# The seam between head attention and output attention: order of the first signs, extremes in three parts, a buffer cleared later, values in smaller first groups

## The chip, the core and the metric

The kernel runs on one core of a Trainium2 chip. The metric is the device time of one execution in microseconds (us); the median of several runs is compared. Engines: TensorE (PE in the profile, PEld its weight loads), VectorE (DVE), ScalarE (ACT), GpSimd (POOL) and SyncE (SP), the last two also issuing DMAs. Each engine takes its instructions from a queue in order.

## What is computed

Four graph layers over 4096 nodes with 64 features and a dense 4096 x 4096 matrix of edges. Each layer adds its result to x. The change lies in the first layer, a graph attention with eight heads of 32 features, whose results are joined and go through one more attention (the "output attention"):

```python
h = maximum(_layernorm(x), 0)
e_s = leaky_relu(f1[:, :, None] + f2[:, None, :], 0.2)      # per head
h_s = elu(softmax(where(mask, e_s, NEG)) @ Wh_s)            # six heads from h, two from intent embeddings
h = concatenate(heads)                                      # 4096 x 256
Who = h @ W_out                                             # 4096 x 64
o1, o2 = Who @ a_out[:64], Who @ a_out[64:]
e_o = leaky_relu(o1[:, None] + o2[None, :], 0.2)
x = x + tanh(softmax(where(mask, e_o, NEG)) @ Who)
```

The other three layers (a hyperbolic attention, a mean over neighbours, a weighted list of the last neighbours) follow.

## The kernel before, in words

Nodes lie in 32 blocks of 128 (NB = 32), a block on the 128 partitions. The kernel never forms the softmax matrix. Since leaky_relu has two slopes, exp(leaky_relu(s + t)) is one of two products of a factor of the row and a factor of the column, and the sign of s + t tells which. So for each pair of blocks `split_edges` (L1227 to L1257) makes a tile of signs `st` (two instructions on ACT, L1242, or now and then on DVE, L1236), masks the edges with it (B, L1248, DVE), and, except for "whole" pairs, takes the other edges (C, L1256, DVE). TensorE then multiplies B and C by the values, scaled with the column factors. For a whole pair it multiplies all edges and takes B off again with negated values.

*Heads.* Two halves of the target nodes, eight heads in each: 16 units. `finish_unit` (L1740) is a generator that turns a unit's sums into elu(...) in steps: transposes (L1751), the division (L1781, nm), Relu and Exp on ACT (L1786, L1787), elu's last step into x (L1788, DVE). After the fourth and the eighth head it also multiplies by W_out: for four groups of four blocks, transposes of x (L1037), their copies on ACT (L1038), `product` (L1797, pwho) and the addition to `who` on DVE (L1808). `who` holds, for each node, the 64 values, then o1 and o2. Behind the last unit the rest of its generator runs out, then `scores_row(1)` (L1518: pro, a transpose of o1 on TensorE, its copy ro on ACT, its store by SP) and `extremes(1)` (L1526: maximum and minimum of o2 and of the values of 16 blocks, four reductions, L1532, and a change of sign, L1533). `extremes(0)` ran earlier, inside the heads.

*Output attention.* Four units of 1024 target nodes; in each, eight mask tiles `mo` of four source blocks (L2204, loaded by SP, three buffers). Ahead of it, in a group of which `in_order()` keeps the order on each engine: psv, the sum of the values by four products with a matrix of ones (L2061); m3, the joined extremes (L2068); their maximum over partitions on POOL (omax, L1208); td and the two Exps of `fzo` (L2071 to L2073); scale factors; and `parts` (L2080), which for a quarter of the blocks (8) makes the values YB and YC as pairs of float16: a product on DVE (pzo, L2085), a copy on ACT (L2088), a difference on DVE (L2090), and for YB a second copy on ACT (L2093). `factors` (L2095) makes YD1 and YD2, which sum the denominators. `staggered` interleaves such streams a step at a time. Behind the group, YCn, the negated YC of the whole pairs, is made for all of them at once (L2136), and then `radii()` (L1847) prepares scalars of the next layer and clears MOV, a buffer of 128 x 4096 bfloat16 that the next layer fills (L1861, POOL). nto, the negated o2 that the signs need, is made for each half (L2057).

In the loop (L2194 to L2251) each mask tile takes two calls of `split_edges`, the edges in another code for the next layer (nmo, L2217, DVE, stored by POOL, L2220), the products of B, C or mo (L2229, acco) and those of the denominators (L2242, L2248, ddo).

What sets the order: outside `in_order()` a scheduler places the instructions of each engine by the order of issue and estimated times; `behind(...)` keeps what is in it after given instructions. Tiles come from pools with a fixed number of buffers: two for st and C, four for B, two for pzo, so a fifth B waits until TensorE is done with the first. In the schedule of before, twelve signs of the output attention stand on ACT among the last steps of the heads, and two of the four psv on TensorE stand between the transposes of the last unit and one between the last two pwho. MOV's clearing stands on POOL ahead of omax.

Of the kernel before, what the change touches and what calls it, by code (L numbers as in the profile page):

```python
# [10 lines left out]
F32 = mybir.dt.float32  # L11
# [830 lines left out]
def kernel(  # L842
# [235 lines left out]
    with ExitStack() as l0:  # L1078
# [199 lines left out]
        orow_d = [dram.tile([1, HW], F32, name="orow_d") for _ in halves]  # L1278
        mx = spool.tile([P, 2, 4], F32, name="mx")
        fz = lp.tile([P, 2, NB, NH], F32, name="fz")  # L1280
# [203 lines left out]
        with ExitStack() as ha:  # L1484
# [40 lines left out]

            def extremes(i):  # L1526

                t, v = who[:, halves[i], D + 1], who[:, halves[i], 0:D]
                for c, (part, of, ax) in enumerate(
                    ((t, ALU.max, AX.X), (t, ALU.min, AX.X), (v, ALU.max, AX.XY), (v, ALU.min, AX.XY))  # L1530
                ):
                    nc.vector.tensor_reduce(mx[:, i, c : c + 1], part, ax, of)  # L1532
                nc.vector.tensor_scalar(mx[:, i, 1::2], mx[:, i, 1::2], -1.0, None, ALU.mult)  # L1533

            pending = None
            for hf in range(2):
                if hf == 1:
# [8 lines left out]
                for hd in range(NH):  # L1546
# [61 lines left out]
                    for j0 in range(0, NB, 2):  # L1608
# [85 lines left out]
                        if hf == 1 and hd == 1 and j0 == NB // 2:  # L1694
                            with behind(*done_at):
                                scores_row(0)
                                extremes(0)
                    if first:
# [40 lines left out]

                    def finish_unit(hf=hf, hd=hd, ev=ev, fme=fme):  # L1740
                        wh = wn[:, hf * HB : (hf + 1) * HB, hd]

# [43 lines left out]
                        nc.scalar.activation(ng, nm, AF.Relu, scale=-1.0)  # L1786
                        nc.scalar.activation(ng, ng, AF.Exp, scale=-1.0)  # L1787
                        nc.vector.scalar_tensor_tensor(  # L1788
# [5 lines left out]
                        def product(bq):  # L1794
                            pw = ps.tile([P, GB, D + 2], F32, name="pwho", tag="misc")
                            for b in range(GB):
                                nc.tensor.matmul(  # L1797
                                    pw[:, b, :],
                                    lhsT=by_g[:, 3 - bq % 2, b * P : (b + 1) * P],
                                    rhs=rho[:, c, :],  # L1800
                                    start=True,
                                    stop=True,
                                )
                            ws = who[:, hf * HB + bq * GB : hf * HB + (bq + 1) * GB, :]
                            if c == 0:
                                nc.vector.tensor_copy(ws, pw)
                            else:
                                nc.vector.tensor_tensor(ws, ws, pw, ALU.add)  # L1808

                        for bq in range(NS):  # L1810
# [8 lines left out]
                            if bq:  # L1819
                                product(bq - 1)  # L1820
                        yield
                        product(NS - 1)

# [3 lines left out]
            with in_order():  # L1827
                scores_row(1)
                extremes(1)
        ea.close()  # L1830
# [16 lines left out]
        def radii():  # L1847

            nc.vector.scalar_tensor_tensor(rabs, rt, -1.0, rt, ALU.mult, ALU.max)
            nc.vector.reciprocal(sqc, rabs)  # L1850
            nc.vector.tensor_tensor(cc, rt, rt, ALU.mult)
            nc.vector.reciprocal(cc, cc)
            nc.vector.tensor_tensor(c2, cc, cc, ALU.mult)
            nc.vector.tensor_scalar(m2c, cc, -2.0, None, ALU.mult)
            nc.vector.tensor_scalar(s2c, sqc, math.sqrt(2.0) * DIST_S, None, ALU.mult)
            nc.vector.tensor_scalar(p2c, cc, 2.0, None, ALU.mult)
            nc.vector.tensor_scalar(cneg, cc, -1.0, None, ALU.mult)
            nc.vector.tensor_scalar(maxn, rabs, 1.0 - PROJ_EPS, None, ALU.mult)
            nc.vector.tensor_scalar(hrow, rabs, 0.5, None, ALU.mult)
            nc.vector.tensor_copy(ident16, ident)  # L1860
            nc.gpsimd.memset(MOV, 0.0)  # L1861

# [147 lines left out]
        with ExitStack() as ob:  # L2010
# [18 lines left out]
            nc.gpsimd.memset(YD1, 0.0)  # L2029
            nc.gpsimd.memset(YD2, 0.0)  # L2030
            aug = hp.tile([P, NB, C_EL + KX], F16, name="aug")
            meano = hp.tile([P, NK, 2, D], F16, name="meano")
# [23 lines left out]
            for bs in halves:  # L2056
                nc.vector.tensor_scalar(nto[:, bs], tcol[:, bs], -1.0, None, ALU.mult)  # L2057
            with in_order():
                psv = ps.tile([P, 8, D], F32, name="psv", tag="misc")
                for g in range(4):  # L2060
# [6 lines left out]
                    )  # L2067
                nc.vector.tensor_tensor(m3, mx[:, 0], mx[:, 1], ALU.max)  # L2068
                m3 = col_maxs(m3, 4, "omax", hp)
# [8 lines left out]

                def parts(g, i):

                    bs = slice(g * NB // 4, (g + 1) * NB // 4)
                    fq = work.tile([P, NB // 4], F32, name="fq", tag="fq")
                    nc.vector.tensor_scalar(fq, fz[:, i, bs], Qo, None, ALU.mult)
                    pz = work.tile([P, NB // 4, D], F32, name="pzo", tag="pzo")
                    nc.vector.tensor_tensor(pz, vals[:, bs], over(fq, D), ALU.mult)  # L2085
# [6 lines left out]
                    if i == 0:  # L2092
                        nc.scalar.activation(y[:, bs, 1], pz, AF.Copy, scale=LO)  # L2093
                        yield 1

                def factors(i):
# [9 lines left out]

                staggered(parts(0, 0), parts(0, 1), factors(0), factors(1))
                nc.vector.tensor_copy(YD2[:, :, 0:3], YD1[:, :, 3:6])
                for g in range(1, 4):
                    staggered(parts(g, 0), parts(g, 1))  # L2110
                nc.vector.tensor_scalar(
# [22 lines left out]

            YCn = hp.tile([P, NB // 8, 2, 2 * D], F16, name="YCn")
            prepared = nc.vector.tensor_scalar(  # L2136
                YCn,
                YC.rearrange("p (n i) s d -> p n i (s d)", i=2)[:, 1::4],
                -1.0,
                None,  # L2140
                ALU.mult,
            )

            with tc.issue_after(prepared.ins):
                radii()
# [47 lines left out]
            for u in range(4):  # L2193
# [8 lines left out]
                for q in range(NQ):  # L2202
# [3 lines left out]
                    for t in range(0, JT, 2):  # L2206
                        j0 = q * JT + t
                        edges = m[:, t : t + 2, :]
                        whole = j0 // 2 % 4 == 1
                        B, C = split_edges(  # L2210
                            work, srow[:, us], nto[:, j0 : j0 + 2], edges, j0, NB + 1, not whole, 4
                        )
                        B2.append(B)
                        if t:
                            with behind(*done_at):
# [3 lines left out]
                                )  # L2219
                                nc.gpsimd.dma_start(noedge_d[q][u // 2][:, :, hs], nm8)  # L2220
                        products = [(accB, YB[:, j0 : j0 + 2], B), (accC, YC[:, j0 : j0 + 2], C)]
# [997 lines left out]
```

## Time and profile before

| | |
|---|---|
| median of 3 runs | 1922.95 us (1919.16 to 1933.77) |
| profiled execution: its own time | 1918.57 us |
| its span, first to last instruction | 1916.8 us |
| mean granted TensorE clock | 0.962 |
| busy: PE, DVE, ACT, POOL | 1756.7, 1586.0, 1428.3, 120.4 us |
| last head product ends, first output product starts | 915.3, 948.4 us |
| last product of the output attention ends | 1134.7 us |

How to read it: a row of the timeline or of the chain begins with the start and the length in us; "x4" counts instructions, and "[7.73 <-ACT YBo L2093]" is idle time of the engine before the row and what ended it. Rows of the chain of work that ended last give time that the path spent in a step. Rows of waits read: who waited for whom, us in total, times, longest. A row of stretches has a pair of busy time and count for each engine, then the granted clock (1.00 is full rate), the busy share of the DMA engines and GB/s. Line numbers are those of the kernel before.

### The profile page before, as it was taken

How to read it: one execution, taken by the hardware profiler on the slowest of the kernel's cores; microseconds unless marked ns; L12 is line 12 of the kernel's file. 1: busy time of each engine (PE TensorE's matmuls, PEld its weight loads, DVE VectorE, ACT ScalarE, POOL GpSimd, SP SyncE). 2: the span in 40 equal slices, each digit the busy share in tenths (PEclk: the TensorE clock that was granted, in tenths of full speed). 3: DMA queues.
4: the chain of work that ended last, by engine and by line, in shares of the span. 5: the costliest groups of instructions: out<-in, count | busy, mean ns of one | idle time of the engine just before them, and what ended most of it. 6: DMA issues, size and time to landing. Idle time of an engine off the chain costs nothing.

```text
span 1916.8 us, 44651 instructions
## 1 busy us (share of the span) xinstructions
PE 1756.7 (92%) x19374; PEld 818.1 (43%) x19374; DVE 1586.0 (83%) x2457; ACT 1428.3 (75%) x1470; POOL 120.4 (6%) x204
## 2 busy tenths in 40 slices
PE   5889988999999999999699996999999998899998
PEld 3444444444444444444334441333333333455433
DVE  6769999999869987999668876888988777756687
ACT  3768888899878987999578977777777775324565
POOL 2000100010000000000111100000011121110000
PEclk8899999999999999999699996999999999899999
DMA  8956554535411110100455534455543210784496
GB/s 112 178 138 92 112 75 80 134 123 194 161 51 51 52 51 24 57 35 2 123 178 185 187 100 128 139 169 177 178 121 119 72 39 6 276 232 154 154 346 183
DMA packets 145978, 239.09 MB, mean 125 GB/s; under 512 B 16662, under 2 KB 106086, under 8 KB 140230
## 3 DMA queue, kind: packets, MB, share of 16 engines
q1 hardware_dynamic: 131244, 194.02, 30.8%
q0 software_dynamic: 14528, 42.13, 12.5%
q8 instruction: 153, 2.51, 0.5%
q14 instruction: 53, 0.43, 0.1%
HBM read 245.37 MB, written 49.46 MB: 154 GB/s over the span
## 4 chain that ended last, share of the span: by engine, by line
PE 57%; DVE 21%; ACT 13%; issue 6%; DMA 2%; POOL 0%; SPq 0%; DVEq 0%; ACTq 0%; POOLq 0%
PE accj L2443 9%; PE accC L1597 7%; ACT st L1242 7%; DVE B L1248 7%; PE acco L2229 6%; PE accB L1597 3%; PE pv L3022 3%; DVE st L1236 3%; PE pf L2433 3%; PE sacc L3046 3%; PE accD L1597 2%; PE pl L2377 2%; PE pu L2397 2%; PE accL L1597 2%; PE pl L2383 2%
## 5 line engine op out<-in xcount | busy, mean ns | idle before, releaser
L1242 ACT ACTIVATE st<-srow,nt 128x2048 int8<-128x2048 f32 x352 | 683.0, 1994 | 85.4 <-DVE B L1248 84.1
L1248 DVE TENSOR_TENSOR B<-st,mres 128x1024 int32<-128x1024 int32 x256 | 311.5, 1220 | 59.5 <-PE accC L1597 36.7
L1597 PE MATMUL accB<-B,ybh 128*32 128x512 fp8e4 x3072 | 256.0, 381 | 20.3 <-DVE B L1248 20.2
L1597 PEld LDWEIGHTS <-ybh 128*32 128x32 bf16 (+1 forms) x6656 | 179.2, 97 | 212.2 <-issue 55.4
L1597 PE MATMUL accC<-mres,ych 128*32 128x512 fp8e4 x2272 | 228.5, 380 | 0.0
L1597 PE MATMUL accC<-B,ycn 128*32 128x512 fp8e4 x2272 | 228.5, 380 | 0.0
L1597 PE MATMUL accD<-B,ybh 128*32 128x512 fp8e4 x2048 | 208.0, 382 | 2.1 <-DVE h L1733 2.1
L1236 DVE TENSOR_SCALAR st<-srow,nt 128x2048 uint8<-128x2048 f32 x160 | 205.3, 1284 | 1.8
L2443 PE MATMUL accj<-sg,who 128*64 128x512 f32 (+1 forms) x512 | 196.9, 614 | 5.1 <-DVE sg L2436 4.8
L2443 PE MATMUL acci<-sg,who 128*64 128x512 f32 (+1 forms) x512 | 196.8, 614 | 0.0
L2399 ACT ACTIVATE yt<-pu,consts 128x512 f32<-128x512 f32 x144 | 98.5, 686 | 99.2 <-PE pu L2398 95.0
L2388 ACT ACTIVATE sg<-pl,rb 128x512 f32<-128x512 f32 x256 | 160.9, 679 | 10.2 <-PE pl L2383 7.5
L1597 PEld LDWEIGHTS <-ych 128*32 128x32 f16 x4096 | 118.3, 97 | 116.7 <-issue 12.1
L1597 PE MATMUL accL<-B,ybh 128*32 128x512 fp8e4 x1536 | 156.8, 384 | 4.3 <-DVE h L1732 4.3
L972 DVE SCALAR_TENSOR_TENSOR raw<-raw 128x1024 f32<-128x1024 f32 x128 | 153.8, 1215 | 0.0
L1242 ACT ACTIVATE st<-srowo,nto 128x1024 int8<-128x1024 f32 x128 | 137.9, 1138 | 19.0 <-DVE B L1248 13.3
L1256 DVE TENSOR_TENSOR C<-B,mres 128x1024 int32<-128x1024 int32 x114 | 139.5, 1224 | 3.1
L3036 ACT ACTIVATE w3b<-pv 128x512 int16<-128x512 f32 x172 | 90.9, 596 | 55.7 <-ACT w3b L3036 23.2
L1597 PE MATMUL accC<-C,ych 128*32 128x512 fp8e4 x1824 | 124.9, 383 | 6.3 <-DVE C L1256 6.2
L2377 PE MATMUL pl<-nm,noid 128*128 128x512 fp8e4 x256 | 82.2, 389 | 16.3 <-ACT sg L2388 14.6
L1597 PEld LDWEIGHTS <-ycn 128*32 128x32 f16 x2272 | 66.7, 97 | 60.1 <-issue 1.0
L2417 DVE SCALAR_TENSOR_TENSOR yt<-sqy,yt 128x1024 f32<-128x1024 f32 x72 | 84.8, 1218 | 5.3 <-ACT sqy L2409 5.2
(540 smaller groups left out, 2721.2 us busy)
## 6 DMA issues: line engine op xcount, KB each, us to landing
raw<-in_adj_dram SPq DMA_DIRECT2D x128, 512.0 KB, 4.7
mo<-edges SPq DMA_DIRECT2D x32, 512.0 KB, 4.1
noedge<-nmo POOLq DMA_DIRECT2D x32, 512.0 KB, 3.6
nm<-noedge SPq DMA_DIRECT2D x64, 256.0 KB, 3.1
m<-edges SPq DMA_DIRECT2D x32, 512.0 KB, 6.2
srow<-srow_d SPq DMA_DIRECT2D x15, 1024.0 KB, 8.2
mres<-in_adj_dram POOLq DMA_DIRECT2D x8, 1024.0 KB, 36.0
edges<-in_adj_dram POOLq DMA_DIRECT2D x8, 1024.0 KB, 14.9
```

What stands on the lines that cost most here:

```text
L972: nc.vector.scalar_tensor_tensor(raw, raw, 0.0, raw, ALU.is_gt, ALU.not_equal, accum_out=bad[:, c : c + 1])
L1236: nc.vector.tensor_scalar(st[:, i, :].bitcast(U8), srow, negs[:, i : i + 1], EDGE, ALU.is_gt, ALU.mult)
L1242: nc.scalar.activation(st[:, i, :], srow, AF.Sign, bias=negs[:, i : i + 1], scale=-1.0)
L1248: nc.vector.tensor_tensor(B.bitcast(I32), st.bitcast(I32), edges.bitcast(I32), ALU.bitwise_and)
L1256: nc.vector.tensor_tensor(C.bitcast(I32), B.bitcast(I32), edges.bitcast(I32), ALU.bitwise_xor)
L1597: ins = nc.tensor.matmul(acc[k * O : (k + 1) * O, :], lhsT=values, rhs=moving(k), start=start, stop=stop,)
L2229: sums = nc.tensor.matmul(acc[k], lhsT=Y[:, i].rearrange("p s d -> p (s d)"), rhs=E[:, i, k * G : (k + 1) * G], start=j0 + i == 0, stop=ac ...
L2377: nc.tensor.matmul(pl, lhsT=noid, rhs=nm[:, b, :].bitcast(F8), start=True, stop=False)
L2388: nc.scalar.activation(sg[:, b0 + k, :], pl, AF.Sigmoid, bias=rb[:, j : j + 1], scale=1.0)
L2399: nc.scalar.activation(far[gi, gj][:, b, :], pu, AF.Sigmoid, bias=nb_t, scale=2.0 * DIST_K / (DIST_S * DIST_S),)
L2443: nc.tensor.matmul(acc[r : r + n, :], lhsT=XQ[:, src, cols], rhs=w, start=start, stop=stop)
L3036: nc.scalar.activation(wk, pvs[i, k], AF.Relu)
```

## The change

Six edits. The extremes of the second half are taken in two parts: of the first 12 of its blocks inside the last unit's `finish_unit`, ahead of its last product, and of the last 4 behind it; mx has three parts and m3 is a reduction over them. The first two calls of `split_edges` in the output attention come after the last Exp of the heads. psv comes after the last `product` and is taken out of the group that is kept in order. MOV is cleared in the second unit, behind the store of its first nmo. The first group of values is cut into blocks 0 to 1 and 2 to 7 (8 blocks in one before). YCn is made one pair of blocks at a time, behind the YC of its group, in place of all at once at the end, and `radii()` follows the last of them.

```diff
-            def extremes(i):
+            def extremes(i, bs):
-                t, v = who[:, halves[i], D + 1], who[:, halves[i], 0:D]
+                t, v = who[:, bs, D + 1], who[:, bs, 0:D]
...
-                        nc.scalar.activation(ng, ng, AF.Exp, scale=-1.0)
+                        relieved = nc.scalar.activation(ng, ng, AF.Exp, scale=-1.0)
+                        relieved_at[:] = [relieved.ins]
...
+                            last_product[:] = [made.ins]
...
                         yield
+                        if final:
+                            extremes(1, slice(HB, NB - GB))
                         product(NS - 1)
...
             with in_order():
                 scores_row(1)
-                extremes(1)
+                extremes(2, slice(NB - GB, NB))
+            at_end = (relieved_at[0], last_product[0])
...
             nc.vector.tensor_copy(ident16, ident)
-            nc.gpsimd.memset(MOV, 0.0)
...
-            with in_order():
-                psv = ps.tile([P, 8, D], F32, name="psv", tag="misc")
+            psv = ps.tile([P, 8, D], F32, name="psv", tag="misc")
+            with behind(at_end[1]):
                 for g in range(4):
                     nc.tensor.matmul(
...
-                nc.vector.tensor_tensor(m3, mx[:, 0], mx[:, 1], ALU.max)
+            with in_order():
+                nc.vector.tensor_reduce(m3, mx.rearrange("p i c -> p c i"), AX.X, ALU.max)
...
+                    elif bs.stop % 8 == 0:
+                        b = bs.stop - 6
+                        negated.append(
+                            nc.vector.tensor_scalar(
+                                YCn[:, b // 8],
+                                YC[:, b : b + 2].rearrange("p i s d -> p i (s d)"),
...
-                staggered(parts(0, 0), parts(0, 1), factors(0), factors(1))
+                staggered(parts(slice(0, 2), 0), parts(slice(0, 2), 1))
+                staggered(parts(slice(2, 8), 0), parts(slice(2, 8), 1), factors(0), factors(1))
                 nc.vector.tensor_copy(YD2[:, :, 0:3], YD1[:, :, 3:6])
-                for g in range(1, 4):
-                    staggered(parts(g, 0), parts(g, 1))
+                for b in range(8, NB, 8):
+                    staggered(*(parts(slice(b, b + 8), i) for i in range(2)))
...
-            prepared = nc.vector.tensor_scalar(
-                YCn,
-                YC.rearrange("p (n i) s d -> p n i (s d)", i=2)[:, 1::4],
...
-            with tc.issue_after(prepared.ins):
+            with tc.issue_after(negated[-1].ins):
                 radii()
...
+                        with behind(*(at_end[:1] if u == 0 and j0 < 4 else ())):
+                            B, C = split_edges(
...
-                                nc.gpsimd.dma_start(noedge_d[q][u // 2][:, :, hs], nm8)
+                                kept = nc.gpsimd.dma_start(noedge_d[q][u // 2][:, :, hs], nm8)
+                            if u == 1 and j0 == 2:
+                                with behind(kept.ins):
+                                    nc.gpsimd.memset(MOV, 0.0)
```

In the changed kernel as it is built, the queues differ from before at this seam alone. ACT has Relu and Exp first, then signs and the copies of transposes in turns; ro, two signs and the Exps of fzo stand behind one another, and one sign stands between those Exps and the first value copy. TensorE has the four pwho, then three psv, pro, and the last psv; the products of the output attention come tile by tile, with YCn's and the denominators' in their places. On DVE the B, C and nmo of the tiles behind the first stand among the value groups. SP's order is the same.

More of the change, by code (lines that the diff above doesn't have):

```diff
@@ L1278 @@
         orow_d = [dram.tile([1, HW], F32, name="orow_d") for _ in halves]
-        mx = spool.tile([P, 2, 4], F32, name="mx")
+        mx = spool.tile([P, 3, 4], F32, name="mx")
         fz = lp.tile([P, 2, NB, NH], F32, name="fz")
@@ L1535 @@
             pending = None
+            last_product, relieved_at = [], []
             for hf in range(2):
@@ L1696 @@
                                 scores_row(0)
-                                extremes(0)
+                                extremes(0, halves[0])
                     if first:
@@ L1740, in finish_unit @@
                     def finish_unit(hf=hf, hd=hd, ev=ev, fme=fme):
+                        final = hf == 1 and hd == NH - 1
                         wh = wn[:, hf * HB : (hf + 1) * HB, hd]
@@ L1796, in product @@
                             for b in range(GB):
-                                nc.tensor.matmul(
+                                made = nc.tensor.matmul(
                                     pw[:, b, :],
@@ L2030 @@
             nc.gpsimd.memset(YD2, 0.0)
+            YCn = hp.tile([P, NB // 8, 2, 2 * D], F16, name="YCn")
+            negated = []
             aug = hp.tile([P, NB, C_EL + KX], F16, name="aug")
@@ L2077, with parts @@
                 nc.vector.tensor_scalar(Qo, Qo, VAL, None, ALU.mult)
-                def parts(g, i):
-                    bs = slice(g * NB // 4, (g + 1) * NB // 4)
-                    fq = work.tile([P, NB // 4], F32, name="fq", tag="fq")
+                def parts(bs, i):
+                    n = bs.stop - bs.start
+                    fq = work.tile([P, NB // 4], F32, name="fq", tag="fq")[:, 0:n]
                     nc.vector.tensor_scalar(fq, fz[:, i, bs], Qo, None, ALU.mult)
-                    pz = work.tile([P, NB // 4, D], F32, name="pzo", tag="pzo")
+                    pz = work.tile([P, NB // 4, D], F32, name="pzo", tag="pzo")[:, 0:n]
                     nc.vector.tensor_tensor(pz, vals[:, bs], over(fq, D), ALU.mult)
@@ L2094, in parts @@
                         yield 1
+                    elif bs.stop % 8 == 0:
[4 more added lines that the diff above has]
+                                YC[:, b : b + 2].rearrange("p i s d -> p i (s d)"),
+                                -1.0,
+                                None,
+                                ALU.mult,
+                            )
+                        )
                 def factors(i):
@@ L2132 @@
                 nc.vector.tensor_scalar(bad[:, 4 * NB + 1 : 4 * NB + 2], sp, SPREAD, None, ALU.is_gt)
-            YCn = hp.tile([P, NB // 8, 2, 2 * D], F16, name="YCn")
-            prepared = nc.vector.tensor_scalar(
-                YCn,
-                YC.rearrange("p (n i) s d -> p n i (s d)", i=2)[:, 1::4],
[L2139 to L2142, printed above, removed]
-            with tc.issue_after(prepared.ins):
+            with tc.issue_after(negated[-1].ins):
                 radii()
@@ L2209 @@
                         whole = j0 // 2 % 4 == 1
-                        B, C = split_edges(
-                            work, srow[:, us], nto[:, j0 : j0 + 2], edges, j0, NB + 1, not whole, 4
-                        )
+                        with behind(*(at_end[:1] if u == 0 and j0 < 4 else ())):
+                            B, C = split_edges(
+                                work,
+                                srow[:, us],
+                                nto[:, j0 : j0 + 2],
+                                edges,
+                                j0,
+                                NB + 1,
+                                not whole,
+                                4,
+                            )
                         B2.append(B)
```

## The prediction

> **What bounds the kernel now.** I read the page's slices first, for a place where TensorE rests.
>
> ```profile
> PE   5889988999999999999699996999999998899998
> PEclk8899999999999999999699996999999999899999
> ```
>
> Both rows fall to 6 in slice 20 (910 to 958 us). That is the seam where the heads end and the output attention begins, and all that the change touches lies there. Next, the busy time by stretch.
>
> ```profile
> 915.30:948.40 33.10, 18.04 (x77) 13.01 (x70) 20.86 (x50) 18.86 (x26) 8.77 (x9) 0.60 0.59 177
> 948.40:961.11 12.71, 7.59 (x25) 2.82 (x25) 11.90 (x30) 6.87 (x14) 0.00 (x0) 0.77 0.01 2
> 961.11:968.46 7.35, 7.35 (x44) 2.14 (x45) 4.30 (x22) 3.96 (x5) 0.73 (x1) 0.63 0.29 94
> 968.46:996.34 27.88, 27.88 (x189) 11.47 (x186) 17.13 (x27) 24.09 (x24) 4.23 (x6) 1.00 0.65 212
> ```
>
> The columns are window, length, busy PE, PEld, DVE, ACT and POOL, then the granted clock. From 968.46 TensorE is busy without a gap at clock 1.00: what is won before that point moves everything behind it. Before it there are 33.1 us from the last head product to the first output product, and 20.06 us (948.40 to 968.46) for two tiles of masks that later take 5.40 + 4.54 = 9.94 us (968.46 to 978.40). The waits of TensorE name the two ends:
>
> ```profile
> PE acco L2229 <- ACT YBo L2093: 7.7, 1, 7.7
> PE tr L1037 <- DVE x L1788: 6.0, 1, 6.0
> PE acco L2229 <- DVE YCn L2136: 5.1, 1, 5.1
> ```
>
> The chain that ended last, and two lines of the timeline, show what stands in the way:
>
> ```profile
> 919.78 2.19 ACT st L1242 x2
> 921.97 0.52 ACT h L1786
> 922.48 1.04 ACT st L1242
> 923.52 0.52 ACT h L1787
> ...
> 934.64 1.81 PE psv L2061 x2
> 936.45 1.62 PE pwho L1797 x8
> 938.09 0.44 DVE who L1808
> 938.55 2.52 DVE mx L1532 x4
> 941.08 2.44 DVE nto L2057
> 943.85 0.40 POOL omax L1208
> ```
>
> ```profile
> 939.95 3.54 POOL L1861 MEMSET MOV<- 128x4096 bf16 x1
> 940.99 2.53 DVE L2057 TENSOR_SCALAR nto<-who 128x16 f32<-128x16 f32 x1
> ```
>
> Three signs (st) stand ahead of the heads' last Relu and Exp, a psv product ahead of the last pwho, and nto, some 0.2 us of work, ends with the clearing of MOV at 943.5.
>
> **The change part by part.** Times are those of the profiled execution: 1918.57 us, span 1916.8. The instruction order of the changed kernel is taken as built; I schedule it forward with durations of rows.
>
> *Signs behind the last Exp.* nm still ends at 919.70. Relu then runs at 919.75, Exp at 920.38 and x (L1788) at 921.04 in place of 924.08. The next copy of transposes had stood behind three signs (923.95 to 927.16); now it waits for one sign pair only: from x to the first pwho 2.65 us in place of 3.60. Gain 3.04 + 0.95 = 3.99. The delayed signs cost nothing: ACT idles 1.44, 0.86 and 3.24 us between 928 and 939, and twelve signs are still done by the first product.
>
> *psv behind the last product.* Between the third and the fourth pwho one psv of 1.81 goes. pwho then ends at 932.16 (938.05 before): gain 5.89 so far. But now three psv stand in a row on TensorE's queue, ahead of pro (the transpose for the score row). At the cold rate of the row above they take 3 x 1.78 = 5.34 after the last pwho's issue, so pro runs at 937.29, not right after who (which would be about 933.4). ACT's queue holds ro (the copy of pro), then two signs (1.07 each), then the Exps of fzo: they can't start before 937.99 + 2 x 1.07 = 940.05.
>
> *Extremes in three parts, MOV away.* Reductions of 12 blocks now run before the last who. The 16-block ones took 2.52 together; from 1.21 (1024 elements) and 0.69 (512) I take 0.95 for 768 and 0.41 for 256. They hold the last who until 932.93 (0.75 late). Then come 4-block reductions (0.85), nto at its bare 0.17, two B and one C (0.61 each, which the order puts between) and m3, at 936.18; before, 943.58. omax and td follow: td at 936.88 in place of 944.27, 7.39 earlier. That is 3.2 us before ACT can take it: ro, not the extremes, now sets Exp, at 940.05 against 944.55. Gain 4.50 here.
>
> *Small first groups.* From Exp to the first product 3.85 us passed, with passes over 512 elements (0.69 on DVE, 0.62 on ACT). Two blocks are 128 elements: 0.30 on ACT (meano's row, 128x128), 0.28 on DVE between 0.17 (32) and 0.43 (256). One sign (1.07) stands before them on ACT. I get 2.40: first product at 942.45, gain 5.95.
>
> *YCn in four pieces, six blocks in the second group.* The first YCn is ready at 945.1; TensorE asks for it at 948.2, and YD2 is ready at 946.4. So the wait of 5.12 us goes, and with it the second cold stretch (961.11 to about 967). What stays is one cold start of 4.6 us (948.40 until about 953.0 in the row). The two mask tiles take 9.94 + 2.1 = 12.03 us in place of 20.06: gain 8.03. Three more negations cost DVE some 0.5 us.
>
> *What is late next.* B, C and nmo of the next tiles now stand between the value groups on DVE, and signs between value copies on ACT. DVE works without rest from 945 to 966. Forward, each value group is ready 4 to 5 us before its products; the tightest is B of blocks 18 and 19, at 965.99 when TensorE asks at 966.04. A slip there passes through one for one: up to 2 us lost. Later stretches have ACT 24.09 of 27.88 and DVE 17.13: no limit.
>
> *MOV in the second unit.* The clearing (3.54) moves on POOL past omax and eight noedge transfers, behind the ninth. That one was issued at 1001.74, so it would fill 1002.45 to 1005.99 of the old time; the next noedge is issued at 1007.98, behind it. DVE then has two B, and one tensor_scalar at 1005.58 that could be held 0.4 us. MOV's first reader is 160 us away. Cost 0; bounds 0 and 3.54. [...]
>
> SP's queue keeps its order: the store of ro and the two score rows behind it (needed in the third unit) start about 1 us earlier.
>
> Sum: 5.95 + 8.03 = 13.98, so 1918.57 - 14.0 = 1904.6. This execution lies 4.4 us below the median of 1922.95, which three runs from 1919.16 to 1933.77 make. The middle of all four is 1921.1; I take that as base: **1907 us**.
>
> **The rivals.**
>
> *A: ro does not hold Exp.* Three dense psv might bring the clock up, and end at the 0.88 each of the early rows (from 916.61): pro 2.7 earlier. Exp then follows td: gain 14.0 + 2.6 = 16.6; if the clock also stays up until the products, 2.1 more, 18.7: 1921 - 17.6 = 1903. Against it: from 925 to 940 TensorE was busy 13.7 of 15 us and the clock stayed at 0.50. [...]
>
> *B: only the start is gained.* If value copies and signs hold each other up on ACT, TensorE starts at 942 but waits in the first tiles as before. Gain 4 to 8: 1915. For it: DVE has no rest for 21 us. Against: 4 us of room at every group.
>
> *C: slower.* ACT carries ten signs among the values of the last three groups. Should every one land before a copy that DVE waits for, DVE's walk grows by 10 x 1.07 = 10.7 us; TensorE then waits over three tiles and returns to half clock as after 955.99, at some 2.3 us for each of three restarts: 17.6 lost against 14.0 gained, so 1925. It decides once the hold-ups pass about 7 us. Against: six pairs of signs are ready in advance, and forward no sign holds a copy more than 1 us.
>
> *D: nothing moves* (DMA or another engine sets the first unit): 1921. Against: the mask transfers land 4.1 us after issue and the fourth is released at the end of the first tile.
>
> **How the numbers follow.** Forecast (gain 10 to 15.5) 0.62; A 0.18; B 0.13; C 0.04; D 0.03. One per cent is about what a measurement of this kernel can tell from no change, here 19 us. The forecast lies within it; A reaches it on a high base or a low run: faster 0.13. C and the scatter of the runs leave 0.05 for slower. The likeliest case alone spans 1903 (1918.57 - 15.5) to 1913 (1922.95 - 10); with A and B, 1900 to 1918.
>
> **What would show it.** In the profile after: x (the heads' last elu) some 3 us after nm less than before; no psv among pwho; nto at 0.2 us; ro on ACT late, with fzo's Exp 2 us behind it and td waiting (right) or not (A); first YBo product near 942; no wait for YCn; from there TensorE without gaps, the third tile's products near 954.5 in place of 968.5. I am wrong if TensorE waits for YBo or B in the tiles behind the first, if the clock is 0.50 beyond 947, or if the output attention ends (1134.7 before) other than near 1120.7.

## The result, and the profile after

The changed kernel took **1906.07 us** (median of 4 runs, 1905.47 to 1907.93), the kernel before 1921.06 us beside it (4 runs, 1919.08 to 1933.77): a ratio of 0.9913, 95% interval 0.9891 to 0.9935. Forecast was 1907, a change within one per cent. The profiled execution took 1907.93 us, span 1906.2.

Below, T is the start of the last head product (accC from em and meanq): 915.14 us in the profile before, 921.37 in the one after. Times "from T" compare the seam between executions whose heads took unequal time. The slices of the page after:

```profile
PE   5789988999999998999899986999999998899998
PEclk8899999999999999999899997999999999999999
```

Slice 20 (the first rows had 6 and 6 there) now shows 8 and 8. The stretches from T to the first output product, the first two tiles, and three further tiles (columns as in the view of before):

```profile
921.37:945.44 24.07, 14.78 (x81) 11.12 (x78) 17.03 (x54) 17.80 (x25) 5.72 (x8) 0.86 0.70 192
945.44:957.06 11.62, 11.62 (x68) 4.46 (x69) 11.07 (x31) 7.10 (x13) 0.00 (x0) 0.85 0.46 152
957.06:972.55 15.49, 15.49 (x108) 6.22 (x105) 15.13 (x45) 14.97 (x20) 2.15 (x3) 1.00 0.60 202
```

The first row, 24.07, stands against 33.26 before and the second, 11.62, against 20.06; TensorE is busy for all of the 11.62. TensorE's waits from the last head product to the end of the output attention:

```profile
PE acco L2252 <- ACT YBo L2102: 4.6, 1, 4.6
PE tr L1037 <- DVE x L1791: 4.6, 1, 4.6
PE acco L2252 <- DVE evD L2286: 1.5, 3, 0.8
PE acco L2295 <- DVE emo L2288: 0.5, 1, 0.5
```

The wait for YCn is gone; a wait for emo is new. And the stretch of the timeline where the chain had gone through the extremes:

```profile
937.05 2.79 PE L2069 MATMUL psv<-who,ones 128*128 128x512 f32 x6
...
940.42 0.17 DVE L2065 TENSOR_SCALAR nto<-who 128x16 f32<-128x16 f32 x1
...
940.81 0.24 ACT L1523 COPY ro<-pro 16x128 f32<-16x128 f32 x1
940.95 2.18 ACT L1242 ACTIVATE st<-srowo,nto 128x1024 int8<-128x1024 f32 x2
...
942.82 0.25 DVE L2080 TENSOR_SCALAR td<-who,omax 128x32 f32<-128x32 f32 x1 [0.29 <-POOL omax L1208]
...
943.11 0.23 ACT L2081 ACTIVATE fzo<-td 128x32 f32<-128x32 f32 x1
```

nto takes 0.17 (2.53 before). The psv after the last pwho run at 0.88 each, and td and ro's two signs end within 0.1 us of each other, at 943.07 and 943.13, where the Exp starts at 943.11: it is a tie. The chain that ended last goes through td in this profile, from the last who by the reductions, B, C, nto, m3 and omax.

| from T, us | before | forecast | after | after, second profile | YCn made once, see below |
|---|---|---|---|---|---|
| x starts | 8.94 | 5.90 | 6.09 | 6.09 | 6.08 |
| last pwho ends | 22.91 | 17.02 | 15.84 | 15.84 | 17.35 |
| ro ends | 24.12 | 22.85 | 19.68 | 19.70 | 21.37 |
| td starts | 29.13 | 21.74 | 21.45 | 21.47 | 22.23 |
| first Exp starts | 29.41 | 24.91 | 21.74 | 21.76 | 23.36 |
| first product | 33.26 | 27.31 | 24.07 | 24.09 | 25.64 |
| third tile | 53.32 | 39.34 | 35.69 | 35.71 | 48.28 |

So the seam gave 53.32 - 35.69 = 17.6 us, not 14.0, and the profiled pair differs by 10.6 in span: T is 6.23 later, the seam 17.63 shorter, the rest 0.8 longer. The order of instructions up to T is the same in both kernels. TensorE's clock was at 0.50 for 6.8 us between 200 us and T in the profile before, and for 20.5 us in the one after. Three psv took 2.63 us at clock 1.00 (this profile) and 5.19 at 0.50 (run with signs ahead of Exp, below), about twice as long; by an estimate from that, half of the 13.7 more is lost, 6.8, about the 6.23; between like instructions of the two profiles the delay grows in three steps of 1.4, 3.6 and 1.3 us, and in each of these places (311, 515 and 737 us) the profile after has 6.8 us at 0.50 where the one before has 3.4 or none. In the second profile of the same kernel T was 917.98 and the span 1903.0.

### The profile page after: what moved, and what is told of

It reads as the page before. It is cut to its first block, busy times and chain, and to the rows that moved or that the text cites. A ratio compares the mean times of both kernels' runs of the same rounds, so it can differ in the third digit from the quotient of the medians.

```text
span 1906.2 us, 44668 instructions
## 1 busy us (share of the span) xinstructions
PE 1754.6 (92%) x19374; PEld 818.2 (43%) x19374; DVE 1584.8 (83%) x2471; ACT 1427.9 (75%) x1473; POOL 120.8 (6%) x204
## 4 chain that ended last, share of the span: by engine, by line
PE 58%; DVE 21%; ACT 13%; issue 6%; DMA 2%; POOL 0%; SPq 0%; DVEq 0%; ACTq 0%
PE accj L2466 8%; PE accC L1598 8%; ACT st L1242 7%; DVE B L1248 7%; PE acco L2252 6%; PE accB L1598 4%; PE pv L3045 3%; DVE st L1236 3%; PE accD L1598 3%; PE sacc L3069 3%; PE pf L2456 2%; PE pl L2400 2%; PE accL L1598 2%; PE pl L2406 2%; PE pu L2420 2%
## 5 line engine op out<-in xcount | busy, mean ns | idle before, releaser
L2466 PE MATMUL accj<-sg,who 128*64 128x512 f32 (+1 forms) x512 | 195.5, 611 | 5.6 <-DVE sg L2459 5.5
L2466 PE MATMUL acci<-sg,who 128*64 128x512 f32 (+1 forms) x512 | 195.4, 611 | 0.0
L2400 PE MATMUL pl<-nm,noid 128*128 128x512 fp8e4 x256 | 81.4, 385 | 17.7 <-ACT sg L2411 15.8
```

Of the source, the lines that this page charges most:

```text
L2400: nc.tensor.matmul(pl, lhsT=noid, rhs=nm[:, b, :].bitcast(F8), start=True, stop=False)
L2466: nc.tensor.matmul(acc[r : r + n, :], lhsT=XQ[:, src, cols], rhs=w, start=start, stop=stop)
```

## The experiments

To be told apart were the forecast's chain (ro with its two signs sets Exp, and each part is worth what was worked out), rival A (an unbroken run of psv raises the clock), and others that each text names; a theory's number is that of its own text. The first seven runs undo one part of the change or make one part alone. Their whole times, most of them of a single run, are given but don't price a part: from the first product of layer 1 to the end, where the queues are the same, these profiles took from 731.6 to 745.1 us (last section). The times from T do. "Changed" is the changed kernel; the diffs are against it but where the text says otherwise.

**One part undone: psv among the pwho again.**

```
-            with behind(at_end[1]):
+            with in_order():
...
```

> The changed kernel with psv put back where it was (two among the transposes of the last unit, one between the last two pwho, one behind pro). All numbers are us from the start of the last head product (meanq): in the changed kernel's profile the first output product came at 24.1 and the third tile at 35.7, in the kernel before at 33.3 and 53.3. Theory 1 (the chain of work): one psv goes back into the path, so first product some 1.8 to 2.0 later, 26.0, third tile 37.6; the clock rises among the pwho as in the changed kernel. Theory 2 (the clock): it was the unbroken run of transposes and pwho that brought the clock up at 13.9; with psv among them it stays at half rate until the output products, pwho cost 1.9 more, first product 27.8, third tile 40. Theory 3 (the forecast's: psv ahead of ro holds the Exps): ro is free earlier, first product at 24 or sooner.

Measured: first product 24.46 from T, third tile 35.90, 1904.9 us. None of the three texts had that: ro came earlier, at 18.58, as in theory 3, but td only at 21.84, and td then sets the Exp. The clock rose 13.9 after T here too, with psv among the pwho, of which the last two took 1.15 and 1.00. So with the clock up the move of psv is worth 0.2 to 0.4 us; what it is worth at half rate was not run. And in this execution, as in changed, the clock rose before the run of psv: rival A's size did not come from A's reason (on the reason itself see the last section).

**YCn made once, behind all values.**

```
-                    elif bs.stop % 8 == 0:
-                        negated.append(nc.vector.tensor_scalar(YCn[:, b // 8], ...))
...
+            prepared = nc.vector.tensor_scalar(YCn, ... [:, 1::4], -1.0, None, ALU.mult)
...
```

> The changed kernel with YCn made for all pairs at once at the end of the value groups. Us from the last head product. Theory 1: first product unchanged at 24.1; TensorE then waits for YCn until all four groups are done, some 12 us behind the first product, and falls to half clock again; third tile near 44, 8 later than in the changed kernel, and the kernel about 8 us slower than it (ratio to the kernel before about 0.996). Theory 2 (the gain behind the first product came from the clock that was already up): third tile at 38 or sooner.

Measured: 22.64 us for the first two tiles where changed has 11.62, with a wait of 8.2 us for YCn: theory 1, but the third tile came at 48.28, 12.6 later than in changed, where it had 8. The time was 1923.73 us (10 runs, 1914.47 to 1927.96), ratio to before 1.0005 (0.998 to 1.0029); that is 17.7 above changed, more than the stage lost, and in the profile the stretch from layer 1 to the end took 744.8 us, 13 more than in changed. In this execution the clock stayed at 0.50 until 19.2 from T, and the chain is the forecast's, link by link:

```profile
931.06 3.35 PE pwho L1800 x16
934.40 3.61 PE psv L2069 x6
938.01 0.12 PE pro L1521
938.13 0.02 issue
938.16 0.26 ACT ro L1523
938.41 2.09 ACT st L1242 x2
940.50 0.12 ACT fzo L2081
```

With T at 917.05 that puts ro's end at 21.37, 1.5 ahead of the forecast, and the first product at 25.64. Three psv took 3.61 there, not 5.34: the clock rose while they ran.

**YCn in pieces alone** (diff against the kernel before).

```
+                        negated.append(nc.vector.tensor_scalar(YCn[:, b // 8], ...))
...
-            with tc.issue_after(prepared.ins):
+            with tc.issue_after(negated[-1].ins):
```

> The kernel before with one part of the change alone: YCn is negated in four pieces inside the value groups, and the products run tile by tile without waiting for one negation. Times from the start of the last head product (before: first product 33.26, third tile 53.32, so 20.06 for two tiles; with the rest of the change and YCn once: 22.64; with all: 11.62). Theory 1 (the wait for YCn and the cold stretch that it brings are a cost of their own): first product at 33.3, third tile at 45 to 46, so two tiles in 12 to 12.7. Theory 2 (small first groups are needed as well, or TensorE waits for values instead): two tiles in 15 to 18, with a wait for YBo in place of the one for YCn.

```profile
919.82:950.25 30.43, 14.85 (x82) 11.11 (x78) 20.74 (x50) 18.89 (x26) 8.76 (x9) 0.73 0.66 192
950.25:962.14 11.89, 11.89 (x68) 4.53 (x69) 11.35 (x30) 8.06 (x14) 0.72 (x1) 0.83 0.14 46
```

Two tiles in 11.89 instead of 20.06, all of it busy: this part is worth 8.2 us without any other (forecast 8.03), theory 1. The start of 30.43 instead of 33.26 is not the edit's: the clock rose at 17.4 from T, and the last pwho took 1.00 instead of 1.81. It took 1912.8 us (before beside it: 1920.55, 7 runs, 1918.89 to 1925.95).

**Signs ahead of the heads' Exp again.**

```
-                        with behind(*(at_end[:1] if u == 0 and j0 < 4 else ())):
+                        with behind():
```

> The changed kernel with the first two pairs of signs free to stand ahead of the heads' last Relu and Exp. Us from the last head product. Theory 1: three signs are back in the chain; x (the last elu) 3.0 later and the first pwho 0.95 later again, less what the shorter queue behind them gives back (three signs and three masks fewer among the last steps): first product 26.5 to 28, third tile 38 to 40. Theory 2 (the chain is set by ro or omax, ACT's order ahead of them does not count): 24 to 25.

Measured: x at 8.65, ro at 26.26, first product 28.30. That is 2.7 later than with YCn once and 4.2 later than changed, but the clock, at 0.50 until 26.0 here, has its part in both. Up to the first pwho, which both runs reach at half rate, the signs cost 3.56 us (12.25 against 8.69; forecast 3.99). Theory 1's first product (26.5 to 28) was missed by 0.3, its third tile (38 to 40) came, at 39.18. And here, all at half rate, the three psv took 5.19, nearly the forecast's 5.34:

```profile
938.08 5.19 PE psv L2069 x6
943.27 0.12 PE pro L1521
943.40 0.02 issue
943.42 0.26 ACT ro L1523
```

1915.87 us.

**MOV cleared in the seam again.**

```
             nc.vector.tensor_copy(ident16, ident)
+            nc.gpsimd.memset(MOV, 0.0)
```

> The changed kernel with MOV cleared in the preparation again; on POOL it stands ahead of omax. Us from the last head product. Theory 1 (a tensor_scalar of DVE cannot run beside a clearing): the clearing runs from 17.8 to 21.3, nto, which ran at 19.1, ends with it at 21.3 and m3 comes 2.2 later: first product 26.3, third tile 38. Theory 2 (nto's 2.5 us had another cause): nto at 0.2 us and first product at 24.1, or held only by omax behind the clearing, 0.5 later at most.

The clearing and four rows of DVE beside it:

```profile
934.46 3.54 POOL L1868 MEMSET MOV<- 128x4096 bf16 x1
...
935.03 2.99 DVE L2066 TENSOR_SCALAR nto<-who 128x16 f32<-128x16 f32 x1
...
935.11 2.92 DVE L1256 TENSOR_TENSOR C<-B,mo 128x512 int32<-128x512 int32 x1
...
935.72 2.32 DVE L1533 TENSOR_SCALAR mx<-mx 128x2 f32<-128x2 f32 x1
935.78 2.25 DVE L1248 TENSOR_TENSOR B<-st,mo 128x512 int32<-128x512 int32 x1
```

nto starts 0.57 after the clearing and ends with it, at 938.02 against 938.00, and everything behind it on DVE is held. td comes at 23.95, the first product at 26.89: 1.25 later than in the run with YCn once, where the clock rose within 0.2 us of the same place, and 2.8 later than in changed, where it rose 5.2 earlier. So 1.25 is the clearing's. 1919.32 us.

**One first group of eight blocks.**

```
-                staggered(parts(slice(0, 2), 0), parts(slice(0, 2), 1))
-                staggered(parts(slice(2, 8), 0), parts(slice(2, 8), 1), factors(0), factors(1))
+                staggered(parts(slice(0, 8), 0), parts(slice(0, 8), 1), factors(0), factors(1))
```

> The changed kernel with one first value group of eight blocks in place of two and six. All times from the start of the last head product; the changed kernel has its first output product at 24.07 where the clock rose at 13.9, and at 25.64 (run with YCn made once, same start) where it stayed at 0.50 until the output products. Theory 1 (the group's size sets the time from Exp to the first product, forecast at 3.85 against 2.40): first product 1.2 to 1.6 later, so 25.4 with the clock up and 27.1 with it down; third tile 1.3 later than 35.69. Theory 2 (the signs on ACT set it, not the group): first product unchanged, 24.1 or 25.6. Theory 3 (a later start lets the stock of masks grow, so the tiles behind run as dense): the first two tiles take 11.6 or less.

Measured: first product 27.41, from the end of the second Exp 3.07 us; changed has 1.99, YCn once 1.95. So the small group is worth 1.1 us (forecast 1.45). The other 0.7 against the YCn run's 25.64 is ro, 0.7 later, for the clock stayed at 0.50 until 20.5. Two tiles took 11.56. 1908.53 us.

**All extremes behind the last product.**

```
...
-                        if final:
-                            extremes(1, slice(HB, NB - GB))
...
-                extremes(2, slice(NB - GB, NB))
+                extremes(1, halves[1])
```

> The changed kernel with all extremes of the second half behind the last product (mx of two parts; m3 is still one reduction). Times from the start of the last head product. Theory 1 (with ro or the signs setting Exp, the extremes in three parts are worth next to nothing): m3 1.0 to 1.6 later than 20.40, td at about 22.8, ro at 18.6 to 19.4 with the clock up and 21.1 with it down, and the first product no more than 0.3 later than 25.64 if the clock is down. Theory 2 (after the change the chain is who, extremes, m3, td, Exp again): first product 1.2 to 1.7 later, 25.3 to 25.8 with the clock up.

Measured: m3 20.59, ro already at 16.88 (pro came ahead of three psv), first product 24.26, 0.2 later than changed. The three parts are worth next to nothing, as theory 1 had it, but not for its reason: ro is free 2.5 earlier than in changed, td alone sets the Exp, and m3 comes 0.2 later and not 1.0 to 1.6. In changed the reductions of 12 blocks hold the last who, which starts at 17.25 from T there and at 15.86 here, and that takes back what the smaller last reductions save. 1908.0 us.

**The changed kernel a second time.**

> The changed kernel a second time, for another phase of the clock. Times from the start of the last head product. If the order of the seam is all that counts: first product 24.07, third tile 35.69 again. If the clock's windows set 1.6 us of it, as the runs with the same start show: 24.1 where the clock rises at 13.9, or 25.6 with ro at 21.1 and the Exp of fzo at 23.4 where it does not, third tile at 35.7 or 37.3. The whole lies at 1905 to 1908 when layer 1 takes 731.6 to 732.1 and some 8 to 13 more when it takes 740 to 745.

Measured: 24.09 and 35.71, the seam of the first profile to 0.02 us, the clock again up at 13.9. The other case, a rise after 20, did not turn up in a profile of changed. 12 runs: eight at 1904.53 to 1906.66, four at 1915.86 to 1922.51; median 1905.95, ratio 0.9944 (0.9919 to 0.9969).

The last four try to go further: in changed, td and ro's signs set Exp together, so both have to be moved.

**psv behind pro, and B and C of blocks 4 to 7 behind td.**

```
-            at_end = (relieved_at[0], last_product[0])
+            at_end = (relieved_at[0], turned[0])
...
+            with behind(*after):
+                at.append(nc.vector.tensor_tensor(B.bitcast(I32), ...))
...
+                                (based.ins,) if u == 0 and 4 <= j0 < 8 else (),
```

turned holds the transpose in scores_row, based is td's instruction; the last line is the new argument of split_edges.

> The changed kernel with two things more: psv stands behind pro on TensorE (ro comes free at once), and the mask steps B and C of blocks 4 to 7 stand behind td on DVE, out of the way from the last who to m3. Times from the start of the last head product. Theory 1 (Exp waits for the later of td and of ro with two signs, as the traces of the changed kernel show: td 21.45, ro 19.44 to 21.1): td 1.8 earlier, at 19.7; ro at 18.5; first product at 22 to 23, third tile at 33.5 to 35, the whole 1 to 2 us less than the changed kernel, about 1904.5. Theory 2 (the masks held back are then late: TensorE waits for B in the first tiles): first product at 22 to 23, third tile unchanged or later than 35.7, the whole no better.

Measured: td 19.50 and ro 18.14 as theory 1 had it, but the first product at 25.38, which neither theory had. ACT's rows (T is 918.38):

```profile
938.30 0.21 ACT L2083 ACTIVATE fzo<-td 128x32 f32<-128x32 f32 x1
938.84 3.23 ACT L1242 ACTIVATE st<-srowo,nto 128x1024 int8<-128x1024 f32 x3 [0.32 <-DVE B L1249]
941.97 0.28 ACT L2098 CAST YBo<-pzo 128x128 f16<-128x128 f32 x1
```

Exp comes 1.95 earlier than in changed, but of the eleven signs that stand ahead of it in changed only eight still do, and three signs, one in changed, stand between it and the first value copy. Third tile 35.32. 1907.59 us (4 runs, 1904.6 to 1909.48), ratio 0.993 (0.9908 to 0.9952).

**The same masks behind the second value group** (diff against the run above; valued holds the last YCo step of blocks 2 to 7).

```
-                                (based.ins,) if u == 0 and 4 <= j0 < 8 else (),
+                                tuple(valued) if u == 0 and 4 <= j0 < 8 else (),
```

> The run before with the mask steps B and C of blocks 4 to 7 held further back: behind the second value group on DVE, not only behind td; the signs that need their buffers move behind the first two groups with them. (psv stays behind pro.) Times from the start of the last head product. Theory 1 (in that run Exp came 1.95 earlier than in the changed kernel, at 19.92, but three signs of 1.08 on ACT and two B, one C and nmo on DVE had moved from ahead of Exp to between Exp and the first value copy, which began at 23.59 and not at 23.04; behind the values they cost nothing): Exp at 19.9, first product at 21.8 to 22.3, second tile at 27.3 to 28.8, third tile at 32 to 33.6, 2 to 3 less than the changed kernel's 24.07 and 35.69. Theory 2 (the stock of masks is what the first tiles live on: four signs and two B later, TensorE waits for B in the second or third tile): first product as above, third tile at 34.5 or later. Whole: 2 to 3 us less than the changed kernel if the clock's windows fall alike, which scatters more than that.

Measured: values ready at 22.8, but the first product at 24.08, at the end of the four psv (18.68 + 5.56 = 24.24): they stand ahead of it on TensorE. Third tile 34.43, between the theories, 1.3 earlier than changed; no wait for B in the first four tiles. Yet 12 runs had a median of 1915.93 (ten at 1913.38 to 1917.41, two at 1905.74 and 1907.83), ratio 0.9971 (0.9958 to 0.9984): no gain of the whole, see below.

**Behind the first value group.** As above, with valued from blocks 0 and 1.

> As the run above, with B and C of blocks 4 to 7 behind the first value group (two blocks) instead of the second. Times from the start of the last head product. Theory 1: first product the same, 21.8 to 22.3, but the second group then has two signs on ACT and two B and two C on DVE between its copies, 2 to 2.5 us: TensorE waits for YBo of the second group, second tile at 28.5 to 30, third tile 1 to 2 later than the run above. Theory 2 (the masks are what is short): third tile earlier than the run above.

```profile
941.06 1.03 PE L2259 MATMUL acco<-B,YBo 128*128 128x512 fp8e4 x4
941.92 1.03 PE L2259 MATMUL acco<-C,YCo 128*128 128x512 fp8e4 x4
944.81 1.04 PE L2259 MATMUL acco<-B,YBo 128*128 128x512 fp8e4 x4 [1.86 <-ACT YBo L2108]
```

First product 22.77, then the wait for the second group that theory 1 had named; third tile 35.19, 0.8 later than in the run above, where the text had 1 to 2 (the clock rose at 13.9 here and at 22.6 there). 1904.48 us.

**psv divided: two early, two behind pro** (diff against the run with masks behind the second group).

```
-            with behind(at_end[1]):
-                for g in range(4):
+            for g in range(4):
+                with behind(*at_end[1:] if g > 1 else ()):
```

> The run with the masks behind the second value group, with psv divided: its first two products (blocks 0 to 15, whose who is old) are free to run while TensorE idles under the heads' last Relu and Exp, the other two stand behind pro. Times from the start of the last head product. In the two runs with all four psv behind pro, they ended at 22.9 (clock up) and 24.2 (clock down), and the first product followed at once (22.77, 24.08), though its values were ready at 22.1 and 22.8: psv had become the last thing ahead of it. Theory 1 (so it is): the two psv end at about 21, first product at 22.1 with the clock up, 22.9 with it down. Theory 2 (values, not TensorE, then set the third tile: its YBo was ready at 33.5 in the run with masks behind the second group): third tile at 33.0 to 33.8, not earlier, against 35.69 in the changed kernel. Theory 3 (a step earlier brings nothing because the rest of the kernel is set by where the clock's windows fall): the whole not less than the changed kernel's 1904.5 to 1906.7; by theories 1 and 2 it is 1902.5 to 1905 in executions of the short kind.

Measured: psv ends at 21.92 and the first product, at 22.52, now waits for its values (ready at 22.46); third tile 34.00, 0.2 behind theory 2, sixth tile 49.97 (changed: 51.18). By the sixth tile 1.2 us of the gain are left. The time, 1907.37 (6 runs, 1901.93 to 1916.64; ratio to before 0.9926, 0.99 to 0.9953), can't be told from changed's.

## Why the prediction came out right

The total came out right: the medians differ by 15.0 us in the first set and by 13.7 where it ran a second time (1919.67 and 1905.95), against 14.0. Its mechanism holds for the largest part; one price was too high, so the seam gave 17.6, more than the range of 10 to 15.5. That the number of the whole agrees to 1 us is in part luck: in the profiled pair later heads took 6.2 of the 17.6, and of the twelve later runs of the same kernel four took 9 us and more longer than the other eight.

- *Signs behind the last Exp.* x 2.85 and the first pwho 3.85 earlier; forecast 3.04 and 3.99. Right.
- *psv.* This is the step that failed, by size: "three psv stand in a row" at the cold 1.78 each, 5.34 together. They took 2.63 in changed, where the clock rose at 13.9 from T, as the third pwho began, and 3.61 where it rose only at 19.2; 5.19 where it rose at 26.0. So the price is that of a psv at half rate, and the clock did not stay there. Exp started 3.2 or 1.6 ahead of the 24.91 forecast. (The sum 937.99 + 2 x 1.07 is 940.13, and 940.05 was written; 0.08 changes nothing.) That ro holds Exp, not the extremes, was right where the clock stayed down (the chain above) and a tie where it rose.
- *Extremes and MOV.* nto 0.17 and td 21.45, forecast 0.17 and 21.74. The last who was held 1.4 us by the reductions, not 0.75, and omax took 0.76 where the row before had 0.39; an earlier last pwho made up for both. Undone, the clearing costs 1.25, the three parts 0.2.
- *Small groups.* From the start of Exp to the first product 2.33, forecast 2.40.
- *YCn and the tiles.* 11.62 for two tiles, forecast 12.03; a gain of 8.44, forecast 8.03. Alone it gave 8.2; left out of the change, it cost 11.0.
- *What is late next.* No wait for YBo behind the first product nor for B or C: right.
- *MOV in the second unit at no cost.* It ran behind the ninth noedge transfer, as forecast, but the prediction read 1001.74 as the ninth's issue, which is the tenth's; the ninth's was 995.67. So the clearing met another tensor_scalar than the one named, emo:

```profile
986.11 3.60 POOL L2243 MEMSET MOV<- 128x4096 bf16 x1
989.16 0.83 DVE L2288 TENSOR_SCALAR emo<-evD 128x512 f16<-128x512 f32 x1
```

emo took 0.83 and, in the second profile, 0.94 in place of 0.42, and TensorE waited 0.5 and 0.6 for it, not at all with MOV back in the seam. Small, and inside the bounds.
- *Rivals.* Rival A's size came (17.6, it had 16.6 to 18.7), not by its reason: the clock was up before the psv ran. B, C and D fall with the profile after: TensorE has no gap in the two tiles, 11.62 of 11.62 us, and no wait for values or masks behind them.
- The last product of the output attention ended at 1124.64, not near 1120.7, for T was 6.2 late; in the second profile, with T 2.8 late, at 1121.21. From T that is 16.3 us sooner than before, so 1.3 of the seam's 17.6 were lost again by then.

## What to carry to other kernels

Where an engine stands idle for a small derived operand, cut that operand in the pieces in which it is consumed: one negation made at once cost 8 to 11 us here, the rest of the seam's 17.6 being 7 to 9, with the clock's part in it. When an instruction is moved out of the way, look at what then stands next on each queue: three times here (signs between Exp and the values, psv ahead of the products, masks in the second group) the gain went to whatever had been moved. And measure a stage from an event inside the same execution: the heads' scatter of 6 us was larger than most parts of this change.

## What the runs showed of the hardware

**The clock.** In the profiles before and after, TensorE's clock is 1.00 or 0.50, and each stretch from one change to the next is a whole number of 3.413 us long (3.41, 6.83, 10.24, 13.65 and more). The offset of this grid differs between executions: one change lies at 922.24 in the profile before and one at 928.41 in the one after, 1.81 windows apart. How many busy windows lie ahead of a rise differs for the transposes and pwho of this seam. Two executions with the same order of instructions up to the values, in stretches of one window each (set within 0.13 us of the grid), the changed kernel's second profile and then the run with a first group of eight:

```profile
924.94:928.35 3.41, 3.41 (x16) 3.05 (x17) 1.38 (x2) 3.41 (x6) 0.00 (x0) 0.52 0.85 277
928.35:931.76 3.41, 3.41 (x18) 3.27 (x18) 1.71 (x4) 2.47 (x3) 0.00 (x0) 0.50 0.61 132
931.76:935.18 3.42, 3.42 (x22) 2.70 (x21) 2.69 (x6) 3.10 (x4) 1.78 (x3) 0.98 0.67 155
```

```profile
926.19:929.61 3.42, 3.42 (x16) 3.20 (x17) 1.38 (x2) 3.42 (x6) 0.00 (x0) 0.50 0.85 270
929.61:933.02 3.41, 3.41 (x18) 3.27 (x18) 1.70 (x4) 2.48 (x3) 0.00 (x0) 0.50 0.58 130
933.02:936.43 3.41, 3.41 (x19) 3.41 (x17) 1.91 (x5) 3.08 (x4) 0.73 (x1) 0.50 0.63 146
936.43:939.85 3.42, 3.42 (x6) 1.43 (x6) 3.42 (x13) 1.78 (x2) 1.62 (x3) 0.51 0.65 180
```

TensorE (second figure) is busy without a gap in both, as far as the profile shows it; the clock (third from the end) rises after two windows in the one and after four in the other. Where products of 512 columns filled a window in the seam or the first two tiles, the next window was at 1.00 each time it was looked at (profile before: 949.54 and 963.20; after: 945.47; YCn once: 943.07 and 960.13; a first group of eight: 936.43; masks behind the second group: 937.92). That is not so everywhere: ahead of layer 1 in the profile before, such products fill 1174.82 to 1178.24, and the clock stays at 0.50 until 1188.48. Of the rows that follow, the first pair is psv alone and the window behind it in the run with masks behind the second group, the second pair the first output products in changed and the window behind them:

```profile
937.92:941.33 3.41, 3.41 (x5) 1.35 (x4) 2.47 (x14) 0.92 (x5) 0.45 (x2) 0.50 0.09 22
941.33:944.74 3.41, 3.41 (x13) 1.36 (x12) 3.19 (x10) 2.22 (x7) 0.00 (x0) 1.00 0.70 207
...
945.47:948.88 3.41, 3.41 (x9) 1.21 (x10) 3.14 (x12) 2.30 (x6) 0.00 (x0) 0.50 0.97 330
948.88:952.29 3.41, 3.41 (x29) 1.40 (x27) 3.25 (x9) 1.22 (x4) 0.00 (x0) 1.00 0.09 31
```

In the run with signs ahead of Exp and the one with a first group of eight the clock rose behind such a window of psv too (5.19 and 4.25 us for three psv: most were paid at half rate by then). So a rise behind a window of dense psv, rival A's reason, is seen in three executions; in changed the clock was up before them. Why it rises under the transposes and pwho in some executions and not in others stays open.

**Its place in the rest of the kernel.** From the first product of layer 1 (accj, L2466) to the end, ten of the fourteen profiled executions took 731.6 to 732.8 us, four took 735.1 to 745.1. By the place of that product on the clock's grid, the ten lie at 3.06 to 3.35 or 0.14 to 0.48 of 3.413 us, the four at 0.52, 2.42, 2.71 and 2.80; after it their clock stood at 0.50 for 39 to 62 us, against 28 to 36. The timed runs fall in two groups likewise: changed's second set at 1904.5 to 1906.7 with a mean clock of 0.965 to 0.969, and at 1915.9 to 1922.5 with 0.957 to 0.960. This is an order seen in the profiles, not tested, and its one edge is thin (0.48 and 0.52). It would account for a seam 1.3 us shorter (masks behind the second group) having a longer median, since ten of its twelve runs took 1913 to 1917 us; but their clocks, 0.956 to 0.967, overlap those of the faster group, and which of them began layer 1 where was not recorded.

**Clearings and VectorE.** A tensor_scalar of VectorE that met the clearing on GpSimd was held: nto took 2.99 us in place of 0.17 with MOV back in the seam and ended at 938.02, the clearing at 938.00; emo took 0.83 and 0.94 in place of 0.42, and in the profile after it ended at 989.99, the clearing at 989.71. Beside the clearing in the second unit one B, one C and the copy of evD from PSUM took 0.68 to 0.69, as in the profile before.
